# A fused four-layer network: one MLP tile, one accumulator pool and one PSUM kind moved at the seam of two stages

## The chip, the core and the metric

The kernel runs on one core of a Trainium2 chip. Its time is the device time of one execution in microseconds; the figure of a version is the median of its runs. The engines are TensorE (PE, with its weight loads PEld), VectorE (DVE), ScalarE (ACT), GpSimd (POOL) and SyncE (SP), which here only issues DMAs.

## The reference, cut to what matters

The input is x of 8 x 256 x 128 values. Four layers follow each other, each with a token mixer and an MLP, each added to x after a layer norm. The change lies where the first layer's MLP ends and the second layer's state-space mixer begins:

```
def fp4_quant_dequant(x):                     # blocks of 16 along the last dim
    scale = maximum(max(abs(xb)) / 6, 1e-12)
    return grid(abs(xb / scale)) * sign(xb) * scale

# layer 0, MLP (352 hidden channels, weights quantized in the same way)
xq = fp4(layernorm(x))
h  = silu(xq @ fp4(w_gate).T) * (xq @ fp4(w_up).T)
x  = x + fp4(h) @ fp4(w_down).T

# layer 1, mixer: four blocks, each on layernorm of the block's input
u  = silu(causal_conv4(in_proj(y)) + cb);  dt, B, C = split(u @ Wx.T)
dt = softplus(dt @ Wdt.T + bdt)
for t:  h = exp(dt_t * A) * h + dt_t * B_t * u_t;   y_t = sum_s h * C_t
out = ((y + u * Dp) * silu(z)) @ Wo.T
...                                           # then layers 2 and 3
```

## The kernel before

The 2,048 tokens are four token blocks (tb 0 to 3) of 512, held as x0 to x3 in SBUF. Stage `l0` does layer 0, stage `l1a` the state-space mixer, `l12` and `l23` the rest. Only the seam of `l0` and `l1a` is touched.

In `l0` the order on TensorE is written by hand; the other engines' instructions are ordered by a scheduler. The generator of `l1a` is advanced beside the last steps of `l0` (`following`), so that its first job's front, the norms and the opening of its pools stand there too.

The last block's MLP (tb 3) is run as two halves of two 128-token tiles each, `beside` each other, the second 7 steps behind. A half is: quantize the normed input into `xq` (`fp4`, lines 521 to 538, on VectorE), transpose it (L265) and copy it (L268), two gate matmuls (L722) copied to `g` by ScalarE (L723) and put through silu (L725), two up matmuls (L729) multiplied by `g` into `h` on VectorE (L730), quantize `h` into `hq` (L521 to L538 again, 768 elements per partition), transpose it into `hT`, six down matmuls (L743), and add to x (L746).

One `fp4` on VectorE is, in this order: L521 reduce to block maxima, L522 scale (tensor_scalar), L524 reciprocal, L525 (tensor_scalar), L527 multiply (tensor_tensor, two SBUF inputs), L531 and L532 (tensor_scalars, the exponent into `q_p`), L534 and L536 (scalar_tensor_tensor of `q_p` and the value, two SBUF inputs), L538 multiply by the scale (tensor_tensor, two SBUF inputs).

Stage `l1a` has 16 jobs (4 blocks of the mixer x 4 token blocks), each with 16 states, 256 slots in all. A slot is, with its engine: b rows from DRAM spread over the partitions (L995, SyncE's queue, two states a load), inflow `st = du * b` (L1001, GpSimd, three slots ahead; states 0 to 5 at the start), decay `da = exp(dt * A)` into PSUM (L1007, ScalarE, one slot ahead), scan `st = da * st + ...` (L1012, VectorE: da in PSUM, st in SBUF), and then for even states `st *= c` (L1034, GpSimd) and a sum into the accumulator `y` on TensorE (L1043), for odd ones transposes (L1021) and weighted sums (L1028, VectorE). A job's `front`, 26 slots ahead, makes xn (L893, ScalarE, after statistics on GpSimd, L881 to L888), its transposes (L898), xp (L901), u by four tap matmuls for each of two channel halves (L909, copied by L914), dt and z. In the loop the order of TensorE, VectorE, ScalarE and GpSimd is the program's. At job 0's slots 1 to 6 the norm of x3 for the mixer (`norm`: L238, L240, L246 to L251 on GpSimd, L257) is also stepped through; the first steps of it lie before the loop.

Memory pools are opened and closed as stacks: a pool opened later may lie where an earlier one lay. Its first writers wait for the last users of every pool that lay under any part of it. In SBUF, `l0`, `l0_e` and `l0_f` lie at 111,328 to 229,088 bytes of a partition; `l1a_b` (b and c rows and the 14 states) lies at 111,328 to 193,248, and `l0_f` begins at 191,200 with `hT`. In PSUM, `l0` has kinds mm (banks 0 to 3), acc (4, 5) and ffn (6, 7); `l1a` has mm (0), acc (1) and the pool `l1a_da` with da0 (2, 3), da1 (4, 5) and y (6, 7). The second half of the last MLP takes its PSUM tiles from mm, the first from ffn.

Of the kernel before, what the change touches and what calls it, by code (L numbers as in the profile page):

```python
# [9 lines left out]
F32 = mybir.dt.float32  # L10
# [6 lines left out]
P = 128  # L17
B, S, D = 8, 256, 128
NTB = 4
TB = 512  # L20
NT = TB // P
# [127 lines left out]
def woven(*parts):  # L149

    parts = [[gen, n, 0] for gen, n in parts]
    while parts:
        part = min(parts, key=lambda p: (p[2] + 1) / p[1])
        part[2] += 1
        try:
            next(part[0])
        except StopIteration:
            parts.remove(part)
# [16 lines left out]
def network_kernel(ctx: ExitStack, tc: tile.TileContext, x_in, packs, places, conv_w, out, stages=STAGES):  # L175
# [16 lines left out]
    def mm_tile(name, kind="mm"):  # L192
        return banks[kind].tile([P, TB], F32, tag=kind, name=name)
# [30 lines left out]
    def layer_norm(src, name, dst=None):  # L224

        gen = norm(src, name, dst)
        while True:
            try:
                next(gen)
            except StopIteration as end:  # L230
                return end.value
# [28 lines left out]
    def transposed(src, name, dst=None, kind="mm"):  # L260

        ps = mm_tile(f"tp_{name}", kind)
        k = src.shape[1]
        for i in range(k):
            T.transpose(ps[:, i * P : (i + 1) * P], src[:, i, :], ident)  # L265
        if dst is None:
            dst = tk.tile([P, TB], F32, tag="xnT", name=f"xnT_{name}")[:, : k * P]
        A.copy(dst, ps[:, : k * P])  # L268
        return dst
# [5 lines left out]
    def flat(ap):  # L275
        return ap.rearrange("p i d -> p (i d)")
# [8 lines left out]
    def ts(i, n=P):  # L285
        return slice(i * n, (i + 1) * n)
# [253 lines left out]
    def l0(w, following):  # L540
        with ExitStack() as es:
            psum_banks(es, mm=4, acc=2, ffn=2)

            pool = es.enter_context(tc.tile_pool(name="l0", bufs=2))
            epool = es.enter_context(tc.tile_pool(name="l0_e", bufs=4))
            fpool = es.enter_context(tc.tile_pool(name="l0_f", bufs=1))
            wT, xnTs, qks, vas, kms, ons, shared = {}, {}, {}, {}, {}, {}, {}

            def normal(tb):
                n = f"l0a{tb}"  # L550
                xn = layer_norm(xs[tb], n)
                yield
                yield
                yield
                xnTs[tb] = transposed(xn, n)
                yield
# [133 lines left out]
                    A.copy(wT[name], ps[:, :I0P])  # L690
                    yield

            def mlp(tb, lo=0, hi=NT, kind="ffn"):

                n = f"l0f{tb}" + (f"_{lo}" if lo else "")
                more = "2" if lo else ""
                part = range(lo, hi)
                x = xs[tb]

                def whole(tag, shape):  # L700
                    if (tb, tag) not in shared:
                        shared[tb, tag] = fpool.tile(shape, F32, tag=tag, name=f"{tag}_{n}")
                    return shared[tb, tag]

                room = lambda m: flat(whole("q_p", [P, NT, I0P])[:, lo:hi])[:, : (hi - lo) * m]
                if lo == 0:
                    shared[tb, "xn"] = layer_norm(x, n)
                xn = shared[tb, "xn"]
                yield
                xq = whole("xq", [P, NT, D])[:, lo:hi]  # L710
                yield from fp4(fpool, flat(xn[:, lo:hi]), flat(xq), (hi - lo) * D, f"x{n}", room(D), more)
                yield
                yield
                xqT = transposed(xq, n, kind=kind)
                yield
                yield
                h = whole("h", [P, NT, I0P])
                G.memset(h[:, lo:hi, I0:], 0.0)
                g = whole("g", [P, NT, I0])
                for i in part:  # L720
                    pg = mm_tile(f"g_{n}_{i}", kind)
                    T.matmul(pg[:, :I0], xqT[:, ts(i - lo)], wT["gate"][:, :I0], start=True, stop=True)  # L722
                    A.copy(g[:, i, :], pg[:, :I0])  # L723
                    yield
                A.activation(g[:, lo:hi], g[:, lo:hi], AF.Silu)  # L725
                yield
                for i in part:
                    pu = mm_tile(f"u_{n}_{i}", kind)
                    T.matmul(pu[:, :I0], xqT[:, ts(i - lo)], wT["up"][:, :I0], start=True, stop=True)  # L729
                    V.tensor_tensor(h[:, i, :I0], g[:, i, :], pu[:, :I0], ALU.mult)  # L730
                    yield
                hq = whole("hq", [P, NT, I0P])[:, lo:hi]
                yield from fp4(fpool, flat(h[:, lo:hi]), flat(hq), (hi - lo) * I0P, f"h{n}", room(I0P), more)
                yield
                yield
                hT = whole("hT", [P, 3, TB])
                for c in range(3):
                    transposed(hq[:, :, ts(c)], f"{n}_{c}", hT[:, c, lo * P : hi * P], kind=kind)
                    yield
                ps = mm_tile(f"d_{n}", kind)  # L740
                for i in part:
                    for c in range(3):
                        T.matmul(ps[:, ts(i)], hT[:, c, ts(i)], wT["down"][:, ts(c)], start=c == 0, stop=c == 2)  # L743
                    yield
                to = flat(x[:, lo:hi])
                V.tensor_tensor(to, to, ps[:, lo * P : hi * P], ALU.add)  # L746

            def beside(a, b, lag):

                live = {0: a, lag: b}  # L750
                at = 0
                while live:
                    for k in [k for k in live if k <= at]:
                        if next(live[k], live) is live:
                            del live[k]
                    at += 1
                    yield

            def chain(*gens):
                for gen in gens:  # L760
                    yield from gen

            def skip(gen, n):
                for _ in range(n):
                    next(gen)
                return gen

            def take(gen, n):
                for _ in range(n):
                    next(gen)  # L770
                    yield
# [3 lines left out]
            with tc.manual_schedule(engines={mybir.EngineType.PE}):  # L775
                for tb in range(2):
                    skip(normal(tb), 4)

                first_half = skip(currents(0), 4 + 10 + 8)
                rest = {}  # L780
                for tb in range(NTB + 1):
                    parts = []
                    if tb < NTB:

                        rest[tb] = attention(tb)
                        parts.append((take(rest[tb], 2 * H), 2 * H + 1))
                    if tb == 0:
                        parts.append((chain(first_half, currents(1), normal(2)), 18 + 40 + 4))
                        parts.append((weights(), 24))
                    elif tb < NTB:  # L790
                        ahead = [currents(tb + 1)] if tb + 1 < NTB else []
                        ahead += [normal(tb + 2)] if tb + 2 < NTB else []
                        if ahead:
                            parts.append((chain(*ahead), 40 + 4))
                    if tb == NTB:
                        last = beside(mlp(tb - 1, 0, NT // 2), mlp(tb - 1, NT // 2, NT, "mm"), 7)
                        parts.append((chain(rest[tb - 1], project(tb - 1), last), 7 + 5 + 36))
                    elif tb:
                        parts.append((chain(rest[tb - 1], project(tb - 1), mlp(tb - 1)), 7 + 5 + 37))

                    if tb >= NTB - 1:
                        n = 2 + 40 + 1 if tb < NTB else 2 + 2 + 1
                        parts.append((take(following, n), n + 1))
                    woven(*parts)


    def l1a(w0):
# [10 lines left out]
        with ExitStack() as es:  # L818
# [215 lines left out]
                G.tensor_tensor(st, st, row.unsqueeze(1).to_broadcast([P, 2, TB]), ALU.mult)  # L1034

            def open_sum(job):
                job.yacc = pda.tile([P, 2, TB], F32, tag="y", name=f"y_{job.n}")
                for c in range(2):
                    T.matmul(job.yacc[:, c, :], diags[job.l][:, c, :], job.u[:, c, :], start=True, stop=False)

# [23 lines left out]
            for k in range(NL * NTB):  # L1064
                job = Job()
# [18 lines left out]
            big = es.enter_context(tc.tile_pool(name="l1a_b", bufs=5))  # L1084
            pool = es.enter_context(tc.tile_pool(name="l1a", bufs=1))
            pda = es.enter_context(tc.tile_pool(name="l1a_da", bufs=1, space=bass.MemoryType.PSUM))

            for j in range(2):
                t = pda.tile([P, 2, TB], F32, tag=f"da{j}", name=f"da{j}")
# [38 lines left out]
            with tc.manual_schedule(engines={kinds.PE, kinds.DVE, kinds.Activation, kinds.Pool}):  # L1128
                for g in range(len(slots) + 10):
                    job, s = slot(g)  # L1130
# [35 lines left out]
                    if job and s == 8:  # L1166
                        open_sum(job)
# [455 lines left out]
```

## Time and profile before

| | |
|---|---|
| median of 3 runs | 2045.22 us (2043.93 to 2050.58) |
| profiled execution | 2052.19 us, span 2050.4 us |
| mean granted TensorE clock | 0.876 |
| busy, share of the span | PE 78%, DVE 79%, ACT 53%, POOL 62% |
| last MLP and seam | about 320 to 370 us |
| first and last scan start | 364.25 and 1267.03 us |

A group of instructions is shown as line, engine, operation, output and inputs, shape and count, then busy us and mean ns of one, then the idle time of the engine just before them and who ended it. A row of the timeline has start and duration in us, then the same; neighbours of one line are merged, with their count. PE counts are hardware passes: two for one f32 matmul, some missing. SPq is SyncE's DMA queue. A row about one line or tile gives durations as minimum/median/maximum in ns.

### The profile page before, as it was taken

To read this page: it belongs to the slowest core of one execution; us is meant where nothing else is said; L and a number is where in the kernel's file an instruction comes from. 1 tells how busy PE (TensorE), PEld (TensorE's weight loads), DVE (VectorE), ACT (ScalarE), POOL (GpSimd) and SP (SyncE) were. 2 spreads that over 40 slices of the span, in tenths; PEclk is the share of its full clock that TensorE was granted. 3 is DMA by queue.
4 is the path that set the end of the run, shared out by engine and by line. 5 is a ranking of instruction groups with operands and counts; after the bars stand their busy time and mean duration, and the time that the engine had idled before them with its cause. 6 is when DMAs were issued, how large, how long until landed. Compare 5 with 4: busy or idle time off the path is not lost. (4 is left out here: it accounts for less than half of the span.)

```text
span 2050.4 us, 21148 instructions
## 1 busy us (share of the span) xinstructions
PE 1589.3 (78%) x6829; PEld 947.1 (46%) x6829; DVE 1630.0 (79%) x3009; ACT 1077.4 (53%) x1764; POOL 1266.7 (62%) x920
## 2 busy tenths in 40 slices
PE   4989895587777778877778777789999776794775
PEld 1434443244444444444444343444446575683665
DVE  6775546799999999999999999925655666899996
ACT  2654452676577776667676666522222243463442
POOL 2000101999899998999989999902343545836446
PEclk8999997699888998888898888899999988796887
DMA  4000001433223332233323333100022344220000
GB/s 129 1 1 1 1 2 58 145 107 134 93 105 120 111 125 94 103 115 105 119 103 112 100 112 105 62 1 0 1 74 98 111 150 130 65 72 9 6 6 6
DMA packets 67693, 153.27 MB, mean 75 GB/s; under 512 B 5248, under 2 KB 26368, under 8 KB 67328
## 3 DMA queue, kind: packets, MB, share of 16 engines
q1 hardware_dynamic: 60224, 123.79, 17.9%
q0 software_dynamic: 7360, 28.14, 4.2%
q8 instruction: 54, 0.88, 0.2%
q14 instruction: 55, 0.45, 0.1%
HBM read 142.74 MB, written 9.18 MB: 74 GB/s over the span
## 5 line engine op out<-in xcount | busy, mean ns | idle before, releaser
L1012 DVE TENSOR_TENSOR_SCAN st_l1a<-da,st_l1a 128x1024 f32<-128x1024 f32 x256 | 581.5, 2277 | 49.7 <-ACT da L1007 43.9
L1001 POOL TENSOR_TENSOR st_l1a<-du_l1a,b_l1a 128x1024 f32<-128x1024 f32 x256 | 597.4, 2356 | 21.4 <-DMA b_l1a<-rows_l1a 21.4
L1007 ACT ACTIVATE da<-dt_l1a,na 128x510 f32<-128x510 f32 x512 | 351.2, 689 | 112.9 <-DVE st_l1a L1012 104.2
L1021 PE MATMUL tr_l1a<-w_const,st_l1a 128*128 128x128 f32 x1152 | 201.0, 306 | 185.6 <-DVE yt_l1a L1028 164.2
L1021 PEld LDWEIGHTS tr_l1a<-w_const,st_l1a 128*128 128x128 f32 x1152 | 149.8, 157 | 331.9 <-issue 212.5
L1034 POOL TENSOR_TENSOR st_l1a<-st_l1a,c_l1a 128x1024 f32<-128x1024 f32 x112 | 263.8, 2356 | 60.5 <-DVE st_l1a L1012 60.5
L1043 PE MATMUL y_l1a<-st_l1a,w_const 128*128 128x512 f32 x448 | 243.9, 673 | 0.0
L1028 DVE SCALAR_TENSOR_TENSOR yt_l1a<-tr_l1a,ct_l1a,yt_l1a 128x256 f32<-128x256 f32 x512 | 215.6, 466 | 13.1 <-PE tr_l1a L1021 12.9
L628 PE MATMUL o_l0a<-ex_l0a,va_l0a 128*32 128x256 f32 x512 | 140.6, 401 | 1.9 <-ACT ex_l0a L620 1.9
L909 PE MATMUL u_l1a<-xp,cw 128*128 128x512 f32 x256 | 120.5, 594 | 1.7 <-ACT xp L901 0.9
L1043 PEld LDWEIGHTS y_l1a<-st_l1a,w_const 128*128 128x128 f32 x448 | 88.5, 220 | 66.0 <-issue 66.0
L1235 PE MATMUL h_l1f<-h_l1f,w_l1f 128*128 128x512 f32 x256 | 116.7, 593 | 0.0
L620 ACT ACTIVATE ex_l0a<-s_l0a 128x512 f32<-128x512 f32 x128 | 75.3, 595 | 73.8 <-PE s_l0a L615 73.5
L1508 POOL TENSOR_TENSOR xd<-de,ex_l3f 128x1024 f32<-128x1024 f32 x32 | 65.2, 2056 | 61.1 <-ACT de L1503 61.1
L1543 PE MATMUL wT<-w_const,wa 128*128 128x128 f32 x512 | 73.4, 312 | 22.6 <-ACT wa L1524 17.0
L1239 ACT ACTIVATE h_l1f<-h_l1f,w_l1f 128x512 f32<-128x512 f32 x32 | 22.0, 687 | 120.9 <-PE h_l1f L1235 120.9
L1543 PEld LDWEIGHTS wT<-w_const,wa 128*128 128x128 f32 x512 | 71.1, 226 | 23.9 <-ACT wa L1524 17.4
L1291 POOL TENSOR_TENSOR st_l2a<-st_l2a,qk_l2a 128x512 f32<-128x512 f32 x32 | 40.4, 1268 | 63.1 <-DVE st_l2a L1290 53.6
L1510 POOL TENSOR_TENSOR xd<-xd,ey_l3f 128x1024 f32<-128x1024 f32 x32 | 78.6, 2475 | 0.2
L1235 PEld LDWEIGHTS h_l1f<-h_l1f,w_l1f 128*128 128x128 f32 x256 | 48.6, 190 | 60.2 <-issue 59.2
L386 POOL DMA_INDIRECT we_l2f<-w_l2f,rows_l2f x44 | 45.5, 1034 | 48.5 <-PE y_l2f L419 31.3
L628 PEld LDWEIGHTS o_l0a<-ex_l0a,va_l0a 128*32 128x32 f32 x512 | 47.1, 113 | 59.9 <-issue 34.4
(490 smaller groups left out, 3260.9 us busy)
## 6 DMA issues: line engine op xcount, KB each, us to landing
b_l1a<-rows_l1a SPq DMA_DIRECT2D x128, 512.0 KB, 3.6
c_l1a<-rows_l1a SPq DMA_DIRECT2D x64, 512.0 KB, 4.1
w_l1f<-w_l1f SPq DMA_DIRECT2D x1, 2888.0 KB
in_l2f<-zero SPq DMA_DIRECT2D x4, 704.0 KB, 7.1
w_l1a<-w_l1a SPq DMA_DIRECT2D x4, 572.0 KB, 5.3
cw<-conv_w SPq DMA_DIRECT2D x4, 512.0 KB
xt_l2f<-in_l2f SPq DMA_DIRECT2D x8, 256.0 KB
out_l2f<-yt_l2f SPq DMA_DIRECT2D x8, 256.0 KB, 3.3
```

Source lines behind the costliest of these rows:

```text
L628: T.matmul(po[b, g][32 * j : 32 * j + 32, :S], va[:, 2 * b + kc, h, :], ex[:, ts(kc, S)], start=kc == 0, stop=kc == 1)
L909: T.matmul(seq(ps), cw[:, j, ts(c)], xp[:, :, j : j + S], start=j == 0, stop=j == 3)
L1001: G.tensor_tensor(t, job.du, row.unsqueeze(1).to_broadcast([P, 2, TB]), ALU.mult)
L1007: A.activation(seq(da[:, c, :])[:, :, 1:], seq(job.dt[:, c, :])[:, :, 1:], AF.Exp, scale=rates[job.l][:, k : k + 1])
L1012: V.tensor_tensor_scan(st, flat(das[s % 2]), st, 0.0, ALU.mult, ALU.add)
L1021: T.transpose(ps[:, j * DI + c * P : j * DI + (c + 1) * P], st[:, c, ts(i)], ident)
L1028: V.scalar_tensor_tensor(dst, src, cs, dst, ALU.mult, ALU.add)
L1034: G.tensor_tensor(st, st, row.unsqueeze(1).to_broadcast([P, 2, TB]), ALU.mult)
L1043: T.matmul(job.yacc[:, c, :], ident, job.st[s][:, c, :], start=False, stop=False)
L1235: T.matmul(ps, w(wn)[:, k * HID + c * P : k * HID + (c + 1) * P], h[:, k, :], start=k == 0, stop=k == NC - 1)
L1510: G.tensor_tensor(xd, xd, wide(ey[:, rs].unsqueeze(2), 2, NX, NK), ALU.mult)
L1543: T.matmul(ps[:, ts(c)], wa[:, h, ts(c)], ident, start=h == 0, stop=h == NH - 1)
```

## The change

`xq` of the MLPs is allocated in `l0_e` (a pool beside `l0_f`) instead of `l0_f`; the second half of the last MLP takes its PSUM tiles from ffn, like the first; `y` of `l1a` gets a pool of its own, opened after `l1a_da`.

In the built program `l0_f` then begins at 193,248, which is where `l1a_b` ends, and `l1a_da` holds banks 2 to 5, the new pool 6 and 7. The instructions are the same ones. Their order moves at the seam only:

- VectorE: the two memsets of da stand ahead of tb 3's residual add (L677) instead of behind the MLP; scan 0 (L1012) stands between L536 and L538 of the first half's hq, instead of behind the MLP; first half's L531, L532, L534, L536 move ahead by one place against the second half's L730, L521, L522; the first half's add (L746) stands two places earlier, and two of x3's four L238 stand between the second half's L534, L536 and L538.
- ScalarE: da0 (two L1007) stands ahead of the MLP's first copy; three L893 stand ahead of the second half's xq copy; xp (L901) stands ahead of the hT copies; the table load for L1007 stands behind the two L914.
- TensorE: one L898 stands ahead of the second half's two xq transposes, two behind them, the fourth and the first u (four L909) ahead of the hq transposes.
- GpSimd and SyncE: the same order.

```
-            def mlp(tb, lo=0, hi=NT, kind="ffn"):
+            def mlp(tb, lo=0, hi=NT):
...
-                def whole(tag, shape):
+                def whole(tag, shape, pool=fpool):
                     if (tb, tag) not in shared:
-                        shared[tb, tag] = fpool.tile(shape, F32, tag=tag, name=f"{tag}_{n}")
+                        shared[tb, tag] = pool.tile(shape, F32, tag=tag, name=f"{tag}_{n}", bufs=1)
...
-                xq = whole("xq", [P, NT, D])[:, lo:hi]
+                xq = whole("xq", [P, NT, D], epool)[:, lo:hi]
...
-                    pg = mm_tile(f"g_{n}_{i}", kind)
+                    pg = mm_tile(f"g_{n}_{i}", "ffn")
...
-                        last = beside(mlp(tb - 1, 0, NT // 2), mlp(tb - 1, NT // 2, NT, "mm"), 7)
+                        last = beside(mlp(tb - 1, 0, NT // 2), mlp(tb - 1, NT // 2, NT), 7)
...
-                job.yacc = pda.tile([P, 2, TB], F32, tag="y", name=f"y_{job.n}")
+                job.yacc = py.tile([P, 2, TB], F32, tag="y", name=f"y_{job.n}")
...
+            py = es.enter_context(tc.tile_pool(name="l1a_py", bufs=1, space=bass.MemoryType.PSUM))
```

The places of `kind` in the transposes, the up and the down matmuls change in the same way as in the gate's.

More of the change, by code (lines that the diff above doesn't have):

```diff
@@ L713, in mlp @@
                 yield
-                xqT = transposed(xq, n, kind=kind)
+                xqT = transposed(xq, n, kind="ffn")
                 yield
@@ L727, in mlp @@
                 for i in part:
-                    pu = mm_tile(f"u_{n}_{i}", kind)
+                    pu = mm_tile(f"u_{n}_{i}", "ffn")
                     T.matmul(pu[:, :I0], xqT[:, ts(i - lo)], wT["up"][:, :I0], start=True, stop=True)
@@ L737, in mlp @@
                 for c in range(3):
-                    transposed(hq[:, :, ts(c)], f"{n}_{c}", hT[:, c, lo * P : hi * P], kind=kind)
+                    transposed(hq[:, :, ts(c)], f"{n}_{c}", hT[:, c, lo * P : hi * P], kind="ffn")
                     yield
-                ps = mm_tile(f"d_{n}", kind)
+                ps = mm_tile(f"d_{n}", "ffn")
                 for i in part:
```

## The prediction

> **What bounds the kernel now.** The page came first, for the state-space loop at the middle of the span. VectorE and GpSimd share it; the only long idle time of GpSimd is one wait of 21.4 us for the first b rows, before its first inflow product (L1001).
>
> ```profile
> L1012 DVE TENSOR_TENSOR_SCAN st_l1a<-da,st_l1a 128x1024 f32<-128x1024 f32 x256 | 581.5, 2277 | 49.7 <-ACT da L1007 43.9
> L1001 POOL TENSOR_TENSOR st_l1a<-du_l1a,b_l1a 128x1024 f32<-128x1024 f32 x256 | 597.4, 2356 | 21.4 <-DMA b_l1a<-rows_l1a 21.4
> ```
>
> Then the timeline of each engine from 316 to 402 us, where the last MLP ends and the loop begins. SyncE issues the b rows 0.13 us after the MLP's last matmul ends (356.15 + 1.71 = 357.86), and GpSimd starts 3.88 us after the issue. So the rows are late because of memory that the MLP holds.
>
> ```profile
> 337.58 0.38 PE L265 MATMUL tp_l0f<-w_const,xq_l0f 128*128 128x128 f32 x2
> ...
> 355.25 0.88 PE L265 MATMUL tp_l0f<-w_const,hq_l0f 128*128 128x128 f32 x6 [1.38 <-DVE hq_l0f L538]
> 356.15 1.71 PE L743 MATMUL d_l0f<-wT_down,hT_l0f 128*128 128x128 f32 x12
> ...
> 357.99 1.28 SPq L995 DMA_DIRECT2D b_l1a<-rows_l1a  x3
> ...
> 361.87 13.88 POOL L1001 TENSOR_TENSOR st_l1a<-du_l1a,b_l1a 128x1024 f32<-128x1024 f32 x6 [21.43 <-DMA b_l1a<-rows_l1a]
> ...
> 364.43 3.70 PE L909 MATMUL u_l1a<-xp,cw 128*128 128x512 f32 x8 [0.78 <-ACT u_l1a L914]
> ```
>
> But the first scan (364.25) is not what the loop then waits for. The second scan (370.25) waits for ScalarE's da (L1007), which stands in ScalarE's order behind job 1's u (L914), and that behind TensorE's two u products (L909), which begin after the MLP. From the MLP's last matmul to the second scan are 370.25 - 357.86 = 12.39 us, and every later scan follows in that chain.
>
> ```profile
> 368.16 0.69 ACT L914 ACTIVATE u_l1a<-u_l1a,w_l1a 128x512 f32<-128x512 f32 x1 [3.79 <-PE u_l1a L909]
> 368.75 1.41 ACT L1007 ACTIVATE da<-dt_l1a,na 128x510 f32<-128x510 f32 x2
> ...
> 370.25 2.29 DVE L1012 TENSOR_TENSOR_SCAN st_l1a<-da,st_l1a 128x1024 f32<-128x1024 f32 x1 [2.68 <-ACT da L1007]
> ...
> 392.40 9.04 DVE L257 TENSOR_SCALAR y<-x,mv_l1a,rs_l1a 128x128 f32<-128x128 f32 x4
> ```
>
> The last row decides the forecast. Four tensor_scalars of 0.34 us each (L257 with GpSimd idle, 335.31: four in 1.12 us) take 9.04 us while GpSimd runs its products back to back: each waits for one product to end. The groups by line of VectorE, each shape apart, for 338 to 358 us, give the MLP's quantizer undisturbed:
>
> ```profile
> L527 DVE TENSOR_TENSOR hq_l0f<-h_l0f,rs_hl0f 128x768 f32<-128x768 f32 x2 | 1.9, 958 | 0.1
> L536 DVE SCALAR_TENSOR_TENSOR hq_l0f<-q_p_l0f,hq_l0f 128x768 f32<-128x768 f32 x2 | 1.9, 957 | 0.0
> L534 DVE SCALAR_TENSOR_TENSOR hq_l0f<-q_p_l0f,hq_l0f 128x768 f32<-128x768 f32 x2 | 1.9, 955 | 0.0
> ...
> L538 DVE TENSOR_TENSOR hq_l0f<-hq_l0f,sc_hl0f 128x768 f32<-128x768 f32 x2 | 1.8, 922 | 0.0
> L532 DVE TENSOR_SCALAR q_p_l0f<-q_p_l0f 128x768 f32<-128x768 f32 x2 | 1.1, 558 | 0.0
> ```
>
> And the instructions of L1489 from 1990 to 2015 us: a scalar_tensor_tensor with both inputs in SBUF, as L534 and L536 are, with GpSimd idle (minimum) and running tensor products (median):
>
> ```profile
> L1489 DVE SCALAR_TENSOR_TENSOR h_r_l3f<-eq_l3f x3: 1214/2917/2919, 1990.1 to 2006.2; 128x1024 bf16<-128x1024 bf16 x3
> ```
>
> **Part 1, the rows come earlier.** With xq out of l0_f, the state-space pool waits for the last reader of xq, the second half's two transposes. In the changed order TensorE meets one transpose of xn (L898) ahead of them, and that waits for ScalarE's L893, which starts at 340.47 behind GpSimd's statistics. So they end at about 341.7 instead of 337.96, the rows are issued at 341.85, and GpSimd starts at 341.85 + 3.88 = 345.7, 16.1 us sooner. The rows can't still wait for the MLP: the changed order has scan 0 between the first half's L536 and L538.
>
> **Part 2, edits at no price of their own.** The two memsets of da (0.91 us each) move into VectorE's idle 2.37 us before 320.41; were that cover gone, 1.8 us. Two da activations (1.41) move into ScalarE's idle 13.57 us before 332.73. u's first product (L909, 3.70) moves ahead of the hq transposes into TensorE's idle 7.96 us before 349.36. Both halves in two banks: the second half's gate matmuls find these free (the first half's h is read by 339.44); what delays them is the transposes above, so its silu ends at 344.9 instead of 343.5: 1.4 us.
>
> **Part 3, the MLP's tail without collisions.** VectorE's order has more inside it: scan 0 (2.28) and two of the four statistics (0.4), less L532, which fits ahead (0.56). With the late silu: 1.4 + 2.28 + 0.4 - 0.56 = 3.5 us later at the last matmul.
>
> **Part 4, what is saved behind it.** After that matmul come u's copy (0.69), one product (3.70), its copy (0.69), the table load, now behind it in ScalarE's order (1.28), da (1.41) and handovers (0.15): 7.9 us instead of 12.39, so 4.5 saved. Parts 3 and 4 alone: -1.0 us.
>
> **Part 5, collisions.** From 345.7 GpSimd has eight products ready that wait for nothing late: L1001 for states 0 to 5, L1034 for state 0 (after scan 0) and L1001 for state 6; then it needs statistics that follow the MLP. In VectorE's order, after the first L532, stand 534, 536, 522, [scan 0], 538, [reciprocal], 525, 527, 531, 532, the MLP's add, 534, 536, 538. All but the bracketed ones, the reduce and the add are tensor_scalars or have two SBUF inputs; the scans show no delay beside GpSimd (mean 2277 ns). By L257 and L1489 each is held until a product ends, and the next product waits for it in turn: one for one. Eight products: 7 x 2.31 (13.88/6) + 2.35 = 18.5 us. Seven VectorE steps between them: 0.96 + 0.96 + 0.19 + 0.92 + 0.18 + 0.96 + 0.56 = 4.7, less an overlap of about 0.3 each (four L257 take 9.04, the sum of their own times and the products' is 10.6): 2.6. From 345.9: 367.0. Then 532, add, 534, two statistics, 536, 538, undisturbed: about 4.0. The second half's hq is ready at 371.0 instead of 355.19: 15.8 later, where part 3 had 3.5.
>
> By the Trainium skill, "SBUF — State Buffer", section "Who interferes with whom", the pair of ports is held for the whole instruction and the second to issue blocks fully. The rows agree that it blocks, but show less than the sum; by the rule the 2.1 us of overlap would come on top, some 2 us more than forecast. It speaks against this change.
>
> **Part 6, the rest.** The matmul tail of a half takes 4.51 us after TensorE was idle for 7.96 (349.36 to 353.87) and 2.61 after 1.38 (355.25 to 357.86). TensorE will now be idle over 9 us before the second tail, so I take the slow one: +1.9; the fast one is the other end. And some comes back at L257: its first op is 13.8 us behind the end of scan 2 (378.6 to 392.4), and from that end GpSimd runs six products, 14.0 us; it waits 0.2 instead of 2.15: -1.9. Bounds 0 and -2.3.
>
> Sum: 15.8 + 1.9 - 4.5 - 1.9 = **+11.3 us**. The profiled execution took 2052.19 (span 2050.4 and 1.8 around it), so 2063.5 for one like it; it lay 7.0 above the median of the runs, 2045.22, so against that 2056.5. Lower bound, if only the four tensor_scalars collide (522, 525, 531, 532: 1.2 + 1.2 + 1.2 + 2.3 = 5.9): -1.0 + 5.9 - 1.9 = +3, 2048. Upper: no overlap between step and product (+2.1) and nothing back at L257 (+1.9): +15.3, 2060.5. I stay near the middle because L1489 and L257 are the nearest rows for all the shapes.
>
> **Rivals.** *No collision* (not slower): the f32 steps slip in between the products, or GpSimd yields. For it: some rows with two SBUF inputs beside GpSimd are not stretched. Then parts 3 and 4 hold, -1.0: 2044. It decides if L534 and L536 stay near 0.96 us. *GpSimd's lead is kept* (faster): the loop uses GpSimd 91 to 98% of the time, so a head start of 16 us could end its backlog by the time of L257, whose 9.04 us would shrink to 1.12: -1.0 - 7.9 = -8.9, 2036. It needs both no collision in the MLP and an idle GpSimd at 392 us. Against it: six products must still follow scan 2, as in part 6. *The rows do not move* is excluded by the place of scan 0.
>
> **How the numbers follow.** Collisions 0.80, no collision 0.13, lead kept 0.07. What can be told from no change is 0.3%, 6.1 us: below 2039.1 or above 2051.4. Of the collision case a tenth ends below 2051.4: slower 0.73, same 0.20, faster 0.07. The collision case's own range, 2048 to 2060.5, holds some nine tenths of it, 0.73; to reach 0.8 the range goes down to 2044, into the second case.
>
> **What would show it.** After: the first L1001 near 345.7 with about 5 us of idle before it; L534, L536, L538 and L527 at 2 to 3 us each between 346 and 366; the last d matmul near 375; the second scan near 383 instead of 370; four L257 in about 7 us; from there to the end the same spacing. Quantizer steps near 0.96 us prove part 5 wrong; a second scan before 368 means a gain.

## The result and the profile after

The changed kernel takes **2059.91 us** (median of 6 runs, 2058.89 to 2066.95) beside 2047.36 us (6 runs) for the kernel before: **slower by 0.72%**, ratio 1.0072, 95% interval [1.0057, 1.0087]. The profiled execution after took 2060.07 us, with a span of 2058.3.

Two rows of the page answer to the two shown of before. GpSimd's wait for the first b rows has shrunk from 21.4 to 6.3 us. VectorE's idle time in front of the scans (49.7 before) has not moved.

```profile
L1012 DVE TENSOR_TENSOR_SCAN st_l1a<-da,st_l1a 128x1024 f32<-128x1024 f32 x256 | 581.9, 2279 | 49.6 <-ACT da L1007 47.9
L1001 POOL TENSOR_TENSOR st_l1a<-du_l1a,b_l1a 128x1024 f32<-128x1024 f32 x256 | 601.2, 2371 | 6.3 <-DMA b_l1a<-rows_l1a 6.3
```

The timeline of the seam, after:

```profile
343.21 0.48 PE L898 MATMUL tp_l1a<-w_const,xn_l1a 128*128 128x128 f32 x1 [3.36 <-ACT xn_l1a L893]
343.48 0.63 PE L265 MATMUL tp_l0f<-w_const,xq_l0f 128*128 128x128 f32 x2
344.24 1.28 SPq L995 DMA_DIRECT2D b_l1a<-rows_l1a  x3
344.57 2.71 PE L722 MATMUL g_l0f<-wT_gate,xnT_l0f 128*128 128x352 f32 x4
348.89 16.33 POOL L1001 TENSOR_TENSOR st_l1a<-du_l1a,b_l1a 128x1024 f32<-128x1024 f32 x6 [6.26 <-DMA b_l1a<-rows_l1a]
...
375.02 1.81 PE L265 MATMUL tp_l0f<-w_const,hq_l0f 128*128 128x128 f32 x6 [7.92 <-DVE hq_l0f L538]
376.62 2.88 PE L743 MATMUL d_l0f<-wT_down,hT_l0f 128*128 128x128 f32 x12
380.33 3.70 PE L909 MATMUL u_l1a<-xp,cw 128*128 128x512 f32 x8 [0.83 <-ACT u_l1a L914]
...
387.56 2.29 DVE L1012 TENSOR_TENSOR_SCAN st_l1a<-da,st_l1a 128x1024 f32<-128x1024 f32 x1 [6.81 <-ACT da L1007]
...
409.21 5.63 DVE L257 TENSOR_SCALAR y<-x,mv_l1a,rs_l1a 128x128 f32<-128x128 f32 x4
```

The rows and the products do come early. The MLP's last matmul ends late, at 379.50 instead of 357.86. And the groups of VectorE by line and shape from 345 to 376 us show why:

```profile
L534 DVE SCALAR_TENSOR_TENSOR hq_l0f<-q_p_l0f,hq_l0f 128x768 f32<-128x768 f32 x2 | 3.6, 1812 | 0.0
L532 DVE TENSOR_SCALAR q_p_l0f<-q_p_l0f 128x768 f32<-128x768 f32 x2 | 3.1, 1573 | 0.0
L527 DVE TENSOR_TENSOR hq_l0f<-h_l0f,rs_hl0f 128x768 f32<-128x768 f32 x1 | 3.0, 3040 | 0.0
L522 DVE TENSOR_SCALAR sc_hl0f<-sc_hl0f 128x48 f32<-128x48 f32 x1 | 2.3, 2318 | 0.0
...
L521 DVE TENSOR_REDUCE sc_hl0f<-h_l0f 128x48 f32<-128x768 f32 x1 | 0.9, 940 | 0.0
```

A tensor_scalar on 48 elements (L522) takes 2.32 us, where an undisturbed one takes 0.19. The reduce, in the same stretch, keeps its 0.94. The means hide pairs: L534 is 2.67 beside a product and 0.95 after the last one.

**How the kernels are compared.** The instructions ahead of the seam are the same in all kernels, yet the last attention product on VectorE (L647), which I use as the mark, starts between 316.90 and 320.25 us in the profiles here (317.81 before, 319.97 after). So places are counted from that mark. The table gives them in us: when the second half's hq is ready, when the last down matmul ends, when scan 1 and scan 7 (the first after the norm of x3) start, and the ratio of the times, each to the runs of before recorded with that kernel (their medians lie between 2046.42 and 2048.88).

| kernel | hq ready | last d | scan 1 | scan 7 | ratio to before |
|---|---|---|---|---|---|
| before | 37.38 | 40.04 | 52.44 | 83.55 | 1 |
| after | 54.90 | 59.53 | 67.60 | 94.78 | 1.0072 [1.0057, 1.0087] |
| b_products | 50.67 | 54.23 | 66.63 | 96.17 | 1.0062 [1.0046, 1.0078] |
| a_hold3 | 48.35 | 52.97 | 61.04 | 89.26 | 1.0035 [1.0019, 1.0051] |
| a_hold0 | 40.33 | 44.95 | 55.06 | 85.57 | 1.0016 [1.0005, 1.0027] |
| a_rows_late | 40.33 | 44.95 | 55.06 | 83.97 | 1.0004 [0.9993, 1.0016] |
| b_onein | 40.74 | 44.89 | 60.73 | 89.44 | 1.0045 [1.0029, 1.0061] |
| c1_xn | 39.76 | 43.83 | 51.89 | 82.17 | 0.9989 [0.9971, 1.0007] |
| c3_hq | 39.75 | 43.81 | 46.38 | 79.91 | 0.9999 [0.9982, 1.0016] |
| b_act_norm | 37.37 | 40.04 | 52.44 | 77.08 | 0.9969 [0.9955, 0.9984] |
| c4_best | 39.74 | 43.81 | 46.38 | 74.73 | 0.9975 [0.9961, 0.9990] |
| c5b | 37.40 | 41.82 | 44.30 | 74.20 | 0.9977 [0.9965, 0.9989] |

### The profile page after: what moved, and what is told of

It is laid out like the page before. It is cut to its first block, busy times and chain, and to the rows that moved or that the text cites. A ratio compares the mean times of both kernels' runs of the same rounds, so it can differ in the third digit from the quotient of the medians.

```text
span 2058.3 us, 21148 instructions
## 1 busy us (share of the span) xinstructions
PE 1590.4 (77%) x6829; PEld 947.8 (46%) x6829; DVE 1635.8 (79%) x3009; ACT 1078.6 (52%) x1764; POOL 1269.3 (62%) x920
## 5 line engine op out<-in xcount | busy, mean ns | idle before, releaser
L1012 DVE TENSOR_TENSOR_SCAN st_l1a<-da,st_l1a 128x1024 f32<-128x1024 f32 x256 | 581.9, 2279 | 49.6 <-ACT da L1007 47.9
L1007 ACT ACTIVATE da<-dt_l1a,na 128x510 f32<-128x510 f32 x512 | 351.5, 689 | 110.5 <-DVE st_l1a L1012 101.4
L1021 PE MATMUL tr_l1a<-w_const,st_l1a 128*128 128x128 f32 x1152 | 200.4, 306 | 183.4 <-DVE yt_l1a L1028 163.1
L1021 PEld LDWEIGHTS tr_l1a<-w_const,st_l1a 128*128 128x128 f32 x1152 | 149.3, 156 | 328.4 <-issue 214.8
L909 PE MATMUL u_l1a<-xp,cw 128*128 128x512 f32 x256 | 120.5, 593 | 1.7 <-ACT xp L901 0.9
L1544 PE MATMUL wT<-w_const,wa 128*128 128x128 f32 x512 | 74.4, 314 | 19.9 <-ACT wa L1525 12.7
```

Of the source, the lines that this page charges most:

```text
L909: T.matmul(seq(ps), cw[:, j, ts(c)], xp[:, :, j : j + S], start=j == 0, stop=j == 3)
L1007: A.activation(seq(da[:, c, :])[:, :, 1:], seq(job.dt[:, c, :])[:, :, 1:], AF.Exp, scale=rates[job.l][:, k : k + 1])
L1012: V.tensor_tensor_scan(st, flat(das[s % 2]), st, 0.0, ALU.mult, ALU.add)
L1021: T.transpose(ps[:, j * DI + c * P : j * DI + (c + 1) * P], st[:, c, ts(i)], ident)
L1544: T.matmul(ps[:, ts(c)], wa[:, h, ts(c)], ident, start=h == 0, stop=h == NH - 1)
```

## The experiments

The theory: GpSimd's products and the quantizer's steps hold each other up, and that is the loss. The rivals: the late silu and the new order are the loss (products cost nothing), or the shared banks are.

**b_products: the collision alone.** Before, plus (the first line is in the second job's front and only keeps the tile for the tie):

```
+ job.xn = xn = tk.tile([P, NT, D], F32, tag="xn", name=f"xn_{n}")
...
+ extra = tmp.tile([P, 2, TB], F32, tag="ex", name="extra")
+ G.tensor_copy(extra[:, 0, 0:1], jobs[1].xn[:, 0, 0:1])      # released by xn
+ for k in range(8):
+     G.tensor_tensor(extra, jobs[0].du, jobs[0].u, ALU.mult)
```

> The kernel before, with one thing added: eight more GpSimd products of the size of L1001 (du times u of the first job into a scratch tile that nothing reads), released when ScalarE has written the second job's xn (340.5 to 342.8 us before), so that they stand in GpSimd's idle time beside the end of the MLP, as the early products of the changed kernel do. Nothing of the change itself is in it. Theory A (collision: a GpSimd product and a VectorE step with operands in SBUF hold each other up): the steps of both halves' quantizer from 343.5 on alternate with the products, single steps of 0.95 us are read as 2 to 3 us, the second half's hq is ready at 367 to 371 instead of 355.2, and since the rows and the first scan come behind the MLP here, all of it reaches the end: 11 to 16 us slower than before. Theory B (the loss of the changed kernel comes from the late silu and the new order, the products cost nothing): eight products of 2.36 us are over by 361, before GpSimd's first own product at 361.9: within 1 us of before.

Its timeline, with nothing of the change in the kernel:

```profile
341.79 22.98 POOL L1112 TENSOR_TENSOR extra<-du_l1a,u_l1a 128x1024 f32<-128x1024 f32 x8
341.89 3.06 DVE L527 TENSOR_TENSOR hq_l0f<-h_l0f,rs_hl0f 128x768 f32<-128x768 f32 x1
...
350.11 0.94 DVE L521 TENSOR_REDUCE sc_hl0f<-h_l0f 128x48 f32<-128x768 f32 x1
350.97 2.23 DVE L534 SCALAR_TENSOR_TENSOR hq_l0f<-q_p_l0f,hq_l0f 128x768 f32<-128x768 f32 x1
353.12 2.32 DVE L522 TENSOR_SCALAR sc_hl0f<-sc_hl0f 128x48 f32<-128x48 f32 x1
```

Eight products that fill idle time of GpSimd put hq back by 13.3 us and the time up by 0.62%: the size of the change's loss. Both engines pay: eight products take 22.98 us, 2.87 each, where an undisturbed one takes 2.35. Theory A holds and the rival "products cost nothing" is out. The collision is enough for the loss; whether it is needed, the next two show.

**a_hold0 and a_hold3: no products, three products.** After, plus these lines ahead of the first three inflows (a_hold0) or behind them (a_hold3):

```
+ zero = tmp.tile([P, 1], F32, tag="zero", name="zero")
+ G.tensor_scalar(zero, xs[NTB - 1][:, NT - 1, 0:1], 0.0, None, ALU.mult)
+ first = jobs[0].du[:, 0, 0:1]
+ G.tensor_tensor(first, first, zero, ALU.add)
```

> The changed kernel, with its GpSimd products held back: a tiny GpSimd pair (zero times the last tile of x3, added to one column of du) makes every product wait for the last addition of the MLP (L746). Rows, banks and the order on TensorE stay as changed; no product and no scan runs beside the quantizer. Counted from the last L647 of each profile. Theory A (collision): the quantizer's steps fall back to 0.45 to 0.96 us, hq of the second half is ready 2 to 4 us after before's (the late silu alone), 12 to 15 us ahead of the changed kernel; products from about 4 us after the last d, scan 0 about where before has it: the time within 3 us of before, 9 to 14 us faster than the changed kernel. Theory B (late silu and order): hq stays as late as in the changed kernel within 2 us, and with the products held it is slower still, by 5 us or more over the changed kernel.

> As the kernel with held products, but the first three products go ahead as in the changed kernel and only the fourth waits for the last L746: a dose between none and eight. Scan 0 stands again in the MLP's tail (between L522 and L538 of the quantizer). Theory A (collision, each product costs the quantizer about what it lasts less a small overlap): 3 x 2.0 = 6 us for the products and 2.3 for scan 0, so the second half's hq is ready 8 to 10 us ahead of the changed kernel's less 2, that is 6 to 10 us ahead of it, and 9 to 12 us behind before's; the time lies between the two kernels, 3 to 9 us above before. Theory B: hq as in the changed kernel; the time at or above the changed kernel's. If the cost came with the scan in the tail and not with the products, hq would be as late as in the changed kernel less 2 us.

The groups of VectorE in a_hold0, 338 to 362 us:

```profile
L527 DVE TENSOR_TENSOR hq_l0f<-h_l0f,rs_hl0f 128x768 f32<-128x768 f32 x2 | 1.9, 960 | 0.1
...
L534 DVE SCALAR_TENSOR_TENSOR hq_l0f<-q_p_l0f,hq_l0f 128x768 f32<-128x768 f32 x2 | 1.9, 951 | 0.0
...
L522 DVE TENSOR_SCALAR sc_hl0f<-sc_hl0f 128x48 f32<-128x48 f32 x2 | 0.4, 186 | 0.0
```

Every step is back at its own time, and hq is 14.6 us ahead of the changed kernel's, with the same rows, banks and order on TensorE (2.28 of them are scan 0, which has left the tail too). The first product starts 1.1 us behind the last d, not 4 as expected, since the rows are there already. Dose and answer go together: 0, 3 and 8 products give hq at 40.33, 48.35 and 54.90, and ratios of 1.0016, 1.0035 and 1.0072. Less scan 0, three products put hq back by 5.7 us, and eight by 12.3. Of the 5.7, the three held steps (L532, L534, L536: 6.99 instead of 2.45) are 4.5, that is 1.5 for each product, where 2.0 was expected; most of the rest is VectorE's wait for the first half's d at L746 (1.82 instead of 0.54). About 0.16% stays in a_hold0, which is not collision in the MLP. Its scan 1 is 2.6 us late:

```profile
359.96 1.81 PE L265 MATMUL tp_l0f<-w_const,hq_l0f 128*128 128x128 f32 x6 [3.46 <-DVE hq_l0f L538]
361.56 2.88 PE L743 MATMUL d_l0f<-wT_down,hT_l0f 128*128 128x128 f32 x12
365.27 5.74 PE L909 MATMUL u_l1a<-xp,cw 128*128 128x512 f32 x8 [0.83 <-ACT u_l1a L914]
```

The second u product takes 5.74 us instead of 3.70: the granted clock is 0.5 of full from 359.16 to 369.40. That part can differ between executions: in a_hold3, behind the same slow tail, the clock is back at 372.38, just ahead of this product, which takes 3.70. In a_hold0's profile the sum is +2.95 (hq) + 1.96 (tail of 4.62 instead of 2.66) + 2.04 (u) - 4.33 (the chain behind the last d, as in the changed kernel) = +2.6.

**a_rows_late: banks and order, but late rows.** After, with one line back:

```
- xq = whole("xq", [P, NT, D], epool)[:, lo:hi]
+ xq = whole("xq", [P, NT, D])[:, lo:hi]
```

> The changed kernel with one part undone: xq's tile is back in the pool that the rows' tiles must wait for, the banks stay as changed (y in a pool of its own, both halves in the same two banks). The rows are issued behind the MLP again, so no product and no scan runs beside the quantizer. Theory A (collision): late silu +2 to +3, d to the second scan 7.9 instead of 12.4 (-4.5), nothing else: the second scan 1 to 3 us ahead of before's (from the last L647), the time 0 to 5 us below before. Theory B (the loss lies with the banks: both halves through the same two, and the new order): it keeps the loss, 8 us or more above before.

Rival B is out: with the banks as changed the loss is gone (ratio 1.0004). My own figure missed as well: I expected scan 1 to be 1 to 3 us early, and it is 2.6 late, for the reason just shown (its L909 takes 5.74 too); nor is the time 0 to 5 us below before's.

**c1_xn: the late silu.** a_hold0, plus a tie of the second job's xn to the second half's silu:

```
+ if lo:                                    # in mlp, behind the silu
+     late["g"] = sm.tile([P, NT], F32, tag="late_g", name="late_g", bufs=1)
+     G.tensor_scalar(late["g"], g[:, lo, 0:NT], 0.0, None, ALU.mult)
...
+ if job.k == 1:                            # in front, behind nm
+     G.tensor_tensor(nm, nm, late["g"], ALU.add)
```

> The kernel with all products held (a_hold0), and one more tie: the second job's normed tile xn (L893 on ScalarE, then L898 on TensorE) has to wait for the second half's silu (zero times its output is added to the factors nm). So the four L893 and the L898 no longer stand ahead of the second half's transposes and copies of xq. Theory A (the late silu and the cold tail come from that order, and both are the rest of the loss that is not collision): the silu falls back from +2.9 to 0, the TensorE tail from hq to the last L746 from 4.67 to about 2.7 because less idle lies ahead of it; hq of the second half within 0.5 us of before's (counted from the last L647), the second scan 3 to 5 us ahead of a_hold0's, the time 3 to 5 us below a_hold0's, that is 0 to 2 us below before. Rival (the tail is slow because both halves share two banks, whatever the order): hq back by 2.9, the tail stays at 4.6, the time 2 to 3 us below a_hold0's.

The silu ends at 25.78 from the mark (before 25.67, a_hold0 28.60): the order of L893 and L898 was its whole delay. The time is that of before within what can be told. But hq is only 0.6 us ahead of a_hold0's, 2.4 behind before's where 0.5 was expected, and the tail is 4.06 where 2.7 was. Its timeline (line numbers are some higher than before's):

```profile
349.55 5.40 PE L915 MATMUL u_l1a<-xp,cw 128*128 128x512 f32 x8 [0.87 <-ACT xp L907]
354.79 0.60 PE L265 MATMUL tp_l0f<-w_const,hq_l0f 128*128 128x128 f32 x4
...
357.73 0.42 DVE L750 TENSOR_TENSOR x<-x,d_l0f 128x256 f32<-128x256 f32 x1 [2.62 <-PE d_l0f L747]
...
360.15 1.81 PE L265 MATMUL tp_l0f<-w_const,hq_l0f 128*128 128x128 f32 x6 [2.47 <-DVE hq_l0f L539]
```

The first half's hq was ready at 351.84, but TensorE was in u's product until 354.95 (5.40 us instead of 3.70, at a granted clock of 0.5 from 349.68 to 353.09). So the first half's addition comes late, VectorE waits 2.62 us for it in its order, and the second half's hq behind it. Neither theory had that; the tail was slow again after only 2.47 us of idle TensorE.

**b_act_norm: the collisions that were there before.** Before, with the norm of x3 in the loop (L257) written by ScalarE:

```
- V.tensor_scalar(dst[:, i, :], src[:, i, :], mv[:, i, 0:1], rstd[:, i : i + 1], ALU.subtract, ALU.mult)
+ A.activation(dst[:, i, :], src[:, i, :], AF.Identity, bias=mv[:, i, 0:1], scale=rstd[:, i : i + 1])
```

with two small GpSimd steps that put the bias, -mean * rstd, where the mean was. The generator's `gap` also goes from 3 to 2, so the norm's steps follow each other sooner. In this kernel scan and decay are L1020 and L1015.

> The kernel before with one thing changed, far from the seam: the norm of x3 inside the loop (L257, four VectorE steps of 128x128, 9.04 us beside GpSimd's products against 0.34 us each beside an idle GpSimd) is written by ScalarE instead (activation with scale and bias; two small GpSimd steps more). Theory A (a VectorE step with its operands in SBUF waits for the GpSimd product that is running): VectorE loses those 9 us and gains nothing else in their place, so the scans behind it are 7 to 9 us earlier and the time is 5 to 9 us below before. Theory B (the four are long for another reason, or VectorE waits there anyway): the scans behind move by less than 2 us, and so does the time.

```profile
390.80 2.28 DVE L1020 TENSOR_TENSOR_SCAN st_l1a<-da,st_l1a 128x1024 f32<-128x1024 f32 x1
392.39 1.63 ACT L262 ACTIVATE y<-x,mv_l1a,rs_l1a 128x128 f32<-128x128 f32 x4
397.32 2.29 DVE L1020 TENSOR_TENSOR_SCAN st_l1a<-da,st_l1a 128x1024 f32<-128x1024 f32 x1 [2.41 <-ACT da L1015]
```

9.04 us on VectorE became 1.63 on ScalarE. Scan 7 comes 6.5 us earlier, a little less than the 7 to 9 expected, as VectorE now waits 2.41 us for da there. The time falls by 0.31% (6.3 us, within the 5 to 9 expected), to a median of 2041.29 us. No kernel here gained more.

**b_onein: does any GpSimd instruction collide?** b_products with one input less:

```
-     G.tensor_tensor(extra, jobs[0].du, jobs[0].u, ALU.mult)
+     G.tensor_scalar(extra, jobs[0].du, 1.0, None, ALU.mult)
```

> As b_products, with the eight extra GpSimd instructions made to read one tile instead of two (du times 1.0 into the same scratch tile, a tensor_scalar of 128x1024 instead of a tensor_tensor). How long such an instruction lasts no trace here shows. Theory A (whatever GpSimd runs on tiles in SBUF holds the VectorE steps up): the quantizer's steps last as long as the GpSimd instruction beside them, 2 us or more each, and the time is 5 to 16 us above before, less if the instruction is short. Theory B (only an instruction with two inputs holds them up): every quantizer step keeps its 0.45 to 0.96 us, hq of the second half is ready within 1 us of before's place (counted from the last attention product on VectorE), the time within 2 us of before.

```profile
341.12 21.03 POOL L1112 TENSOR_SCALAR extra<-du_l1a 128x1024 f32<-128x1024 f32 x7
341.22 1.75 DVE L527 TENSOR_TENSOR hq_l0f<-h_l0f,rs_hl0f 128x768 f32<-128x768 f32 x1
...
346.43 0.94 DVE L534 SCALAR_TENSOR_TENSOR hq_l0f<-q_p_l0f,hq_l0f 128x768 f32<-128x768 f32 x1
347.30 1.02 DVE L522 TENSOR_SCALAR sc_hl0f<-sc_hl0f 128x48 f32<-128x48 f32 x1
```

In between both theories. These instructions last longer (2.77 to 3.21 us each) but put hq back by 3.4 us only, a quarter of 13.3. A step that starts just after such an instruction has started is held for about its first 1.0 us (L527: 341.22 + 1.75 - 0.96 = 342.01, 0.9 after its start); most that start later in it run at their own time (L534). One doesn't fit: the second half's L531, 2.2 us behind such a start, takes 1.08 instead of 0.56. The rest of its 0.45% lies elsewhere: the granted clock is 0.5 from 357.46 to 371.11, so the tail is slow (+1.5), and the first u product takes 6.68 us.

**c3_hq, c4_best, c5b: what an early start is worth without collisions.** c3_hq is c1_xn with the products released by the last L538 instead of L746, and with da of slots 1 to 3 ahead of the second job's front on ScalarE. c4_best adds the edit of b_act_norm. c5b has the norm on ScalarE too, releases products and xn by that L538, and puts the front off by two slots. The lines below are c5b's, and the last is in c5b only; in its rows L1021 is the decay and L1026 the scan.

```
+     G.tensor_scalar(late["hq"], hq[:, 0, 0:NT], 0.0, None, ALU.mult)      # in mlp, second half
...
+ G.tensor_tensor(first, first, late["hq"][:, 0:1], ALU.add)                # ahead of the first inflow
...
- for gen in fronts:
+ for gen in fronts if g > 1 else ():                                       # c5b only
```

> As c1_xn, with two more edits that ask what limits the seam once nothing collides: the GpSimd products are released by the last step of the second half's quantizer (hq) instead of by the last L746, and the first decays (da of slots 1 to 3) stand ahead of the next layer's front steps on ScalarE. Theory A: products run beside TensorE's transposes and d matmuls, where VectorE has little to do; the first product starts about 0.6 us after hq, scan 0 about 3.1 us after hq, the second scan within 3 us of the last L746 (before 12.4, changed kernel 8.1); the first four scans are 6 to 10 us ahead of before's and the time is 4 to 9 us below before. Rival (the steps behind the second scan wait for ScalarE's silu, tables and the front of the second job anyway, so an earlier start is lost there): scans 0 and 1 early, scan 4 within 2 us of before's place, the time within 2 us of c1_xn's.

> c3_hq and b_act_norm together: products released by hq, decays ahead of the front, no tie of xn to the first half, and the norm of x3 on ScalarE. If the two gains are independent they add up: 9 to 17 us below before, the fastest of all kernels here. If both only shift the same wait (for instance GpSimd becomes the engine that the scans wait for), the sum is 3 us or more short of that.

> Built on the changed kernel, with what the runs so far point to: products and the second job's xn released by the last quantizer step of the second half (so neither the collisions, nor u's first product ahead of the first half's transposes on TensorE, which put hq 2.4 us back in c1_xn), the second job's front on ScalarE and TensorE put off by two slots of the loop, and the norm of x3 on ScalarE (the one edit of b_act_norm). Theory A (the first scans are paced by what stands ahead of da on ScalarE): hq within 0.6 us of before's (counted from the last attention product), scans 0 to 3 by 4 to 10 us ahead of before's, the gains of this and of the norm on ScalarE add up: 8 to 15 us below before. Rival (a later stretch of the loop takes an early start back, since TensorE and ScalarE of the second job's front come as late as before or later): scans 0 to 3 early, scan 7 no more than 2 us ahead of b_act_norm's, the time within 2 us of b_act_norm's.

All three start the scans early (scan 1 by 6.1 and 8.1 us), and keep 2.4 to 3.6 us of it at scan 7, counted against the kernel with the same norm. None of it is left in the time: c3_hq is level with before, c4_best and c5b are no faster than b_act_norm. The rivals were right about the time, but not about the place: c3_hq's scan 4 is still 6.7 us ahead of before's (within 2 was expected), c5b's scan 7 is 2.9 ahead of b_act_norm's (no more than 2 was expected). In c5b the wait is seen at scan 3: VectorE stands 8.71 us for a da that ScalarE has behind both u products.

```profile
372.84 1.40 ACT L1021 ACTIVATE da<-dt_l1a,na 128x510 f32<-128x510 f32 x2
374.35 2.29 DVE L1026 TENSOR_TENSOR_SCAN st_l1a<-da,st_l1a 128x1024 f32<-128x1024 f32 x1 [8.71 <-ACT da L1021]
```

For c4_best and c5b it goes inside the loop, long after the seam: against b_act_norm they are still 3.8 and 2.3 us ahead at scan 100, and 1.4 and 0.0 behind at scan 255, the last one (all counted from the mark). What takes it there was not settled, nor where c3_hq's goes.

## Why the prediction was right or wrong

The direction, the mechanism and its place were right. What failed are sizes: part 5's term for hq (15.8 forecast, 17.5 measured), part 2's silu, which feeds it (1.4 forecast, 2.95 measured), and part 6's gain at L257 (1.9 forecast, 3.4 measured). The steps, each against the marks of the table:

- **Part 1.** L898 did stand ahead of the transposes. They end at 343.48 + 0.63 = 344.11; less the 2.16 by which the mark is later in this profile, 341.95, against 341.7. The first product came 1.0 us later than forecast (28.92 from the mark against 27.9), since the rows took 4.65 us from issue to start instead of 3.88.
- **Part 2, failed in one term.** The silu came 2.95 us late, not 1.4. The transposes end 0.25 us later than forecast, and the gate matmuls, now behind 3.36 us of idle TensorE, take 2.71 us (shown above) instead of before's 1.45: the granted clock had fallen to 0.5 at 342.58. c1_xn showed the order as the cause of the late silu. u's first product was hidden, as forecast: TensorE then waits 8.80 us for hq. In a_hold0, without collisions, the transposes start 0.38 us behind the first half's hq; in c1_xn, where that hq is ready 2.2 us earlier and the product takes 5.40 us, it costs.

```profile
338.77 1.45 PE L722 MATMUL g_l0f<-wT_gate,xnT_l0f 128*128 128x352 f32 x4 [0.81 <-ACT xnT_l0f L268]
```

- **Part 5, failed in one term.** First half's L532 was to fit ahead of the products. With the later silu it did not: VectorE waited for L730 until 348.63, and L532 met the first product (2.58 us instead of 0.56). So eight steps, not seven, stand between the eight products. The rest went as written: all three forms held, scans and reduces not. First half's L538 keeps its 0.95, but there it is the product that waits (3.07 us instead of 2.35). From the first product's start (348.89) to the end of the last held step (370.96) are 22.07 us, where 21.3 were forecast; eight products of 2.35 and the eight steps' own 5.3 make 24.1, so the overlap was 2.0, as estimated. By the Trainium skill, "SBUF — State Buffer", section "Who interferes with whom", the second to issue blocks fully, and the 2.0 would come on top; the measurement decides for the estimate. With the first product 1.0 us later, hq came 17.5 us late altogether, not 15.8.
- **Part 4 and the slow tail of part 6.** The chain behind the last d took 8.07 (7.9 forecast), and the tail 4.63 instead of 2.66, +1.97 (+1.9 forecast).
- **Part 6, L257, mis-sized.** It gave back 3.4 us (9.04 to 5.63), not 1.9. The first of the four met a product with 0.67 us left (0.76), two met a whole one (2.38 each), and the last ran free (0.34), since GpSimd's order had come to statistics (L881) there.

The misses have opposite signs (+1.7 at hq, -1.5 at L257), so that scan 7 is 94.78 - 83.55 = 11.2 us late, as forecast (+11.3): that the sum agrees is luck. The ratio says more, 0.72% or 14.7 us, with an interval from 11.7 to 17.8. One pair of profiles can't decide that: the same scan 7 gives +12.6 for b_products (ratio: +12.7) and -6.5 for b_act_norm (-6.3), but +5.9 for b_onein (+9.2) and -9.4 for c5b (-4.7). "The same spacing to the end" isn't shown either: counted from the mark, the difference is 9.1 us at the last scan and 5.7 at the end of the profiles (the profile of before took 4.8 us more than the median of its runs, that of after 0.2). The last scan of before starts at 1331.79 us, not at the 1267.03 given ahead of the prediction. What lies between 11.2 and 14.7 stays open. Against the time, 2059.91 beside 2056.5, 2.1 of the 3.4 us come from the baseline: the median of all six runs of before is 2047.36, where the first three gave 2045.22.

The rivals: *no collision* was wrong in its condition, and its price too. a_hold0, which is that case made real, is not 1.0 us ahead of before but 2.6 behind at scan 1, since the silu (1.5 more than forecast), the slow tail (1.9) and, in that profile, the slow u (2.0) belong to it, and the 2.1 net for scan 0, two statistics and L532 do not. *The lead is kept* fell with it; but L257, where it hoped to gain, was worth 0.3% of the time, as b_act_norm showed. (GpSimd's use in the loop, read there as 91 to 98%, is 84% in three of the stretches of 50 us.)

## What to carry to other kernels

Before work is moved to an earlier place, look at what the other engines do there: a GpSimd product beside VectorE's tensor_scalars or steps with two SBUF inputs cost VectorE's path here 1.5 to 1.7 us of its 2.35. The sign is in the profile before the change is made: a short step whose mean becomes that of GpSimd's instruction. The same sign shows where a gain lies, here four steps of 0.34 us that took 9.04 and, moved to ScalarE, gave 0.3% of the time.

## What the runs showed of the hardware

- Which VectorE steps a two-input GpSimd product holds up. Held: tensor_scalar (0.19 to 2.32 us, 0.56 to 2.58), scalar_tensor_tensor with two SBUF inputs (0.95 to 2.67), tensor_tensor with two SBUF inputs (0.96 to 3.06). Not held: reduce (0.94), reciprocal (0.44), the scan with da in PSUM (2.28), tensor_tensor with one input in PSUM (L730, 0.51).
- A GpSimd tensor_scalar of 128x1024 let such a step go 0.9 to 1.3 us after its own start, of 2.8 to 3.2 us, with the one exception above (b_onein). By the same section of the Trainium skill whoever issues first has the ports for the whole instruction; that agrees with the two-input products, and not with this one.
- TensorE's matmul tail ran at full rate after 1.38 us of idle (before) and slow after 2.47 (c1_xn): 2.31 us for twelve passes instead of 1.71. The granted clock in all these traces is 1.0 or 0.5, and every stretch of it a multiple of 3.41 us: 0.5 from 359.92 to 363.33 in c1_xn. In c5b it falls at 356.64, amid the down matmuls, after only 1.47 us of idle, and that tail is slow from its fifth down pass. So the idle time just ahead doesn't decide alone; where such a stretch begins does too. The Trainium skill, "TensorE: Matmul & The Clock Gate", section "What's actually happening", has the clock fall after an idle window of about 3.4 us. The length agrees, but the 3.41 us ahead of these two falls were not idle: TensorE was busy for 1.18 (c1_xn) and 1.80 (c5b) of them. The clock stayed at 0.5 for 3.41 us in c1_xn and for 10.24 in a_rows_late.
